# A convolution with residual and group normalization: from one image in four parities on the full PE array to two images in row parity on four array tiles

## The chip, the cores and the metric

The kernel runs on one core of a Trainium2 chip. The metric is device time in microseconds of one execution, lower is better; "span" is the profiled execution from first to last instruction and is some 1.8 us shorter than the time. PE is the matmul engine (its weight loads are counted apart, as PEld), DVE the vector engine, ACT the scalar engine, POOL the general engine, and the DMA queues move data between memory and the core. A record is one instruction in the trace; a call of `nc.tensor.matmul` in FP32 leaves two (192 for 96 calls in the kernel before). A group is the work for one block of rows of an image or a pair, and a group is called warm when PE's granted clock reads 1.00 during it and a record of 396 columns takes 0.333 us. The chain of waits is the work that ended last, followed back from the last instruction.

## The reference

```python
def _gn(v, G=16, eps=1e-5):          # mean and variance over 2 channels x H x W
    g = v.reshape(B_, G, C_ // G, H_, W_)
    return ((g - m) / jnp.sqrt(s + eps)).reshape(v.shape)

# x: (8, 32, 128, 128) f32, weight: (32, 32, 3, 3), bias: (32,)
x = x + conv(_gn(x), weight, bias)   # convolution by FFT of size 256
```

The FFT convolution crops its result at an offset, so that only a corner of about 66 x 66 outputs per image is a real convolution; elsewhere the output is x plus bias. All of x must still be read and written: 16.8 MB each way.

## The kernel before

The host permutes x so that one image fills 128 partitions as 4 parities (row and column odd or even) x 32 channels, 64 x 64 elements each. Four 128x128 matrices per group of 11 rows do the convolution. Statistics of an image are taken 1 to 2 images ahead.

```python
def multiply(img, n):
    ps = ps_conv.tile([P, ROWS, N], F32, ...)              # 11 x 33 = 363 columns
    for k in range(4):
        top, left = n * ROWS + k // 2, k % 2
        nc.tensor.matmul(ps, w_sb[:, k, :], g[:, top : top + ROWS, left : left + N], ...)
    return ps
...
take_stats(1, 0, NSTAT)
aggregate(1)
for img in range(B):
    more, yet_more = img + 1 < B, img + 2 < B
    ps = multiply(img, 0)
    if more:
        group_mean(img + 1)          # small matmul, its operand is ready long since
        deviations(img + 1)
    add(img, 0, ps)
    if yet_more:
        take_stats(img + 2, 0, NSTAT // 2)     # two images ahead
    ps = multiply(img, 1)
    if more:
        group_variance(img + 1)      # second small matmul
        normalize(img + 1)
        store(img + 1, N, H)
    add(img, 1, ps)
    if yet_more:
        take_stats(img + 2, NSTAT // 2, NSTAT)
        aggregate(img + 2)
    ps = multiply(img, 2)
    add(img, 2, ps)
    store(img, 0, N)
```

Of the kernel before, what the change touches and what calls it, by code (L numbers as in the profile page):

```python
# [21 lines left out]
F32 = mybir.dt.float32  # L25
AF = mybir.ActivationFunctionType
ALU = mybir.AluOpType

P = 128
EPS = 1e-5  # L30
FFT = 256
STATS = 8


@with_exitstack
def conv_preact_kernel(
    ctx: ExitStack,
    tc: tile.TileContext,
    x: bass.AP,
    weight: bass.AP,  # L40
    bias: bass.AP,
    out: bass.AP,
):
    nc = tc.nc

    B, _, H, W = x.shape
    C = P // 4
    LO = (FFT - 2 * H) // 4 - 1
    N = H - LO
    ROWS = 11  # L50
    NCHUNK = N // ROWS
    NSTAT = H // STATS

    cpool = ctx.enter_context(tc.tile_pool(name="const", bufs=1))
    xpool = ctx.enter_context(tc.tile_pool(name="x", bufs=1))
    spool = ctx.enter_context(tc.tile_pool(name="small", bufs=2))
    ps_conv = ctx.enter_context(tc.tile_pool(name="ps_conv", bufs=6, space=bass.MemoryType.PSUM))
    ps_stat = ctx.enter_context(tc.tile_pool(name="ps_stat", bufs=1, space=bass.MemoryType.PSUM))


    xts = [xpool.tile([P, H, W], F32, name=f"x{img}") for img in range(B)]
    w_sb = cpool.tile([P, 4, P], F32, name="w_sb")
    bias_sb = cpool.tile([P, 1], F32, name="bias_sb")
    for img in range(B):
        parts = 4 if img == 0 else 2
        for k in range(parts):
            rows = slice(k * H // parts, (k + 1) * H // parts)
            nc.sync.dma_start(xts[img][:, rows, :], x[img, :, rows, :])  # L68
        if img == 0:
            nc.sync.dma_start(w_sb, weight)  # L70
            nc.scalar.dma_start(bias_sb, bias)


    pair = cpool.tile([P, P // 2, 2], F32, name="pair")
    nc.gpsimd.memset(pair, 0.125)
    nc.gpsimd.affine_select(  # L76
        out=pair, in_=pair, pattern=[[-2, P // 2], [0, 2]], base=0,
        channel_multiplier=1, compare_op=ALU.is_ge, fill=0.0,
    )
    nc.gpsimd.affine_select(  # L80
        out=pair, in_=pair, pattern=[[2, P // 2], [0, 2]], base=1,
        channel_multiplier=-1, compare_op=ALU.is_ge, fill=0.0,
    )
    pair2 = pair.rearrange("p a b -> p (a b)")
    avg = cpool.tile([P, P], F32, name="avg")
    nc.vector.tensor_add(avg[:, 0 : 2 * C], pair2[:, 0 : 2 * C], pair2[:, 2 * C : 4 * C])  # L86
    nc.vector.tensor_add(avg[:, 2 * C : 3 * C], avg[:, 0:C], avg[:, C : 2 * C])
    for k in (0, 1, 3):
        nc.vector.tensor_copy(avg[:, k * C : (k + 1) * C], avg[:, 2 * C : 3 * C])
    eps = cpool.tile([P, 1], F32, name="eps")  # L90
    nc.vector.memset(eps, EPS * FFT * FFT)

    warm = cpool.tile([P, 1], F32, name="warm")
    nc.scalar.activation(warm, eps, AF.Sqrt)  # L94


    gs = []
    for k in range(2):
        g = cpool.tile([P, N + 1, N + 1], F32, name=f"g{k}")
        nc.gpsimd.memset(g[:, N : N + 1, :], 0.0)  # L100
        nc.gpsimd.memset(g[:, 0:N, N : N + 1], 0.0)
        gs.append(g)

    stats = [cpool.tile([P, NSTAT, 6], F32, name=f"stats{img}") for img in range(B)]
    mvs, ps_ms, ps_vs, means = {}, {}, {}, {}

    def take_stats(img, first, last):
        for s in range(first, last):
            nc.vector.bn_stats(  # L109
                stats[img][:, s, :],  # L110
                xts[img][:, STATS * s : STATS * (s + 1), :].rearrange("p h w -> p (h w)"),
            )

    def aggregate(img):
        mvs[img] = spool.tile([P, 2], F32, tag="mv", bufs=3, name=f"mv{img}")
        nc.vector.bn_aggr(mvs[img], stats[img].rearrange("p n s -> p (n s)"))  # L116

    def group_mean(img):
        ps_ms[img] = ps_stat.tile([P, 1], F32, tag="ps_m", name=f"ps_m{img}")
        nc.tensor.matmul(ps_ms[img], avg, mvs[img][:, 0:1], start=True, stop=True)  # L120

    def deviations(img):

        means[img] = spool.tile([P, 2], F32, tag="mean", name=f"mean{img}")
        nc.vector.tensor_copy(means[img][:, 0:1], ps_ms[img])  # L125
        diff = means[img][:, 1:2]
        nc.vector.tensor_sub(diff, mvs[img][:, 0:1], means[img][:, 0:1])  # L127
        nc.vector.scalar_tensor_tensor(  # L128
            diff, in0=diff, scalar=diff, in1=mvs[img][:, 1:2], op0=ALU.mult, op1=ALU.add
        )  # L130

    def group_variance(img):
        ps_vs[img] = ps_stat.tile([P, 1], F32, tag="ps_v", name=f"ps_v{img}")
        nc.tensor.matmul(ps_vs[img], avg, means[img][:, 1:2], start=True, stop=True)  # L134

    def normalize(img):
        xt, g = xts[img], gs[img % 2]

        std = spool.tile([P, 1], F32, tag="std", name=f"std{img}")
        nc.scalar.activation(std, ps_vs[img], AF.Sqrt, bias=eps, scale=float(FFT * FFT))  # L140
        rstd = spool.tile([P, 2], F32, tag="rstd", name=f"rstd{img}")
        nc.vector.reciprocal(rstd[:, 0:1], std)  # L142
        nc.vector.scalar_tensor_tensor(  # L143
            rstd[:, 1:2], in0=means[img][:, 0:1], scalar=-1.0, in1=rstd[:, 0:1],
            op0=ALU.mult, op1=ALU.mult,
        )
        nc.scalar.activation(  # L147
            g[:, 0:N, 0:N], xt[:, LO:H, LO:W], AF.Identity,
            bias=rstd[:, 1:2], scale=rstd[:, 0:1],
        )  # L150

        low = xt[:, N:H, :].rearrange("p h w -> p (h w)")
        nc.scalar.activation(low, low, AF.Identity, bias=bias_sb)  # L153
        right = xt[:, 0:N, N:W]
        nc.scalar.activation(right, right, AF.Identity, bias=bias_sb)  # L155

    def multiply(img, n):
        g = gs[img % 2]
        ps = ps_conv.tile([P, ROWS, N], F32, tag="ps", name=f"ps{img}_{n}")
        for k in range(4):  # L160
            top, left = n * ROWS + k // 2, k % 2
            nc.tensor.matmul(  # L162
                ps, w_sb[:, k, :], g[:, top : top + ROWS, left : left + N],
                start=(k == 0), stop=(k == 3),
            )
        return ps

    def add(img, n, ps):

        part = xts[img][:, n * ROWS : (n + 1) * ROWS, 0:N]  # L170
        nc.vector.scalar_tensor_tensor(  # L171
            part, in0=ps, scalar=bias_sb, in1=part, op0=ALU.add, op1=ALU.add
        )

    def store(img, first, last):
        nc.sync.dma_start(out[img, :, first:last, :], xts[img][:, first:last, :])

    take_stats(0, 0, NSTAT)
    aggregate(0)
    group_mean(0)  # L180
    deviations(0)
    group_variance(0)
    normalize(0)
    store(0, N, H)
    take_stats(1, 0, NSTAT)
    aggregate(1)
    for img in range(B):
        more, yet_more = img + 1 < B, img + 2 < B
        ps = multiply(img, 0)
        if more:  # L190
            group_mean(img + 1)
            deviations(img + 1)
        add(img, 0, ps)
        if yet_more:
            take_stats(img + 2, 0, NSTAT // 2)
        ps = multiply(img, 1)
        if more:
            group_variance(img + 1)
            normalize(img + 1)
            store(img + 1, N, H)  # L200
        add(img, 1, ps)
        if yet_more:
            take_stats(img + 2, NSTAT // 2, NSTAT)
            aggregate(img + 2)
        ps = multiply(img, 2)
        add(img, 2, ps)
        store(img, 0, N)


# [36 lines left out]
```

## Time and profile before

| | before |
|---|---|
| time, median (range) | 89.98 us (89.44 to 90.11, 3 runs) |
| span of the profiled run | 88.2 us |
| PE busy, DVE busy, ACT busy | 67.2, 60.6, 37.9 us |
| PE's convolution on the chain of waits | from 16.4 to 82.4 us without a break |
| moved by DMA | 33.84 MB, 384 GB/s over the span, some 424 GB/s in the middle |

How to read it: the busy times alone suggest that PE has a quarter of the span to spare. The chain of waits says otherwise: from 16.4 us on the convolution never stops, and what PE does not use lies before and behind it. The lines, and how full the transfers are, are in the prediction.

### The profile page before, as it was taken

To read this page: it belongs to the slowest core of one execution; us is meant where nothing else is said; L and a number is where in the kernel's file an instruction comes from. 1 tells how busy PE (TensorE), PEld (TensorE's weight loads), DVE (VectorE), ACT (ScalarE), POOL (GpSimd) and SP (SyncE) were. 2 spreads that over 40 slices of the span, in tenths; PEclk is the share of its full clock that TensorE was granted. 3 is DMA by queue.
4 is the path that set the end of the run, shared out by engine and by line. 5 is a ranking of instruction groups with operands and counts; after the bars stand their busy time and mean duration, and the time that the engine had idled before them with its cause. 6 is when DMAs were issued, how large, how long until landed. Compare 5 with 4: busy or idle time off the path is not lost.

```text
span 88.2 us, 744 instructions
## 1 busy us (share of the span) xinstructions
PE 67.2 (76%) x224; PEld 41.5 (47%) x224; DVE 60.6 (69%) x142; ACT 37.9 (43%) x34; POOL 2.1 (2%) x11
## 2 busy tenths in 40 slices
PE   0000022599999999999999999999999999999300
PEld 0000022356665665666566556656664666666000
DVE  0308965992999799979979997998899723222200
ACT  4200003970049517922980594189139707910000
POOL 6200000000000000000000000000000000000000
PEclk9999999999999999999999999999999999999997
DMA  1679999999999999999999999999999999799392
GB/s 20 160 283 420 441 416 416 424 416 416 416 424 428 428 420 413 424 416 424 405 415 436 428 422 420 422 439 428 423 427 419 437 431 426 306 401 424 153 391 100
DMA packets 5186, 33.84 MB, mean 384 GB/s; under 512 B 704, under 2 KB 704, under 8 KB 2368
## 3 DMA queue, kind: packets, MB, share of 16 engines
q1 hardware_dynamic: 5040, 33.82, 93.1%
q10 hardware_dynamic: 144, 0.00, 0.1%
q8 instruction: 1, 0.02, 0.1%
q14 instruction: 1, 0.01, 0.0%
HBM read 17.04 MB, written 16.78 MB: 384 GB/s over the span
## 4 chain that ended last, share of the span: by engine, by line
PE 76%; DMA 8%; DVE 7%; ACT 2%; issue 1%; SPq 0%; DVEq 0%
PE ps L162 73%; DMA x<-x_dram 8%; DVE stats L109 4%; PE ps_m L120 2%; PE ps_v L134 2%; ACT g L147 1%; DVE x L171 1%; DVE mv L116 0%; SPq L68 0%; ACT std L140 0%; DVE mean L128 0%; DVE rstd L142 0%; DVE rstd L143 0%; DVE mean L127 0%; DVE mean L125 0%
## 5 line engine op out<-in xcount | busy, mean ns | idle before, releaser
L162 PE MATMUL ps<-g,w_sb 128*128 128x363 f32 x192 | 65.9, 493 | 2.1 <-ACT g L147 2.1
L162 PEld LDWEIGHTS ps<-g,w_sb 128*128 128x128 f32 x192 | 36.1, 197 | 23.5 <-ACT g L147 5.2
L109 DVE BATCH_NORM_STATS2 stats<-x 128x6 f32<-128x512 f32 x64 | 39.5, 679 | 3.4 <-DMA x<-x_dram 3.4
L171 DVE SCALAR_TENSOR_TENSOR x<-ps,bias_sb,x 128x363 f32<-128x363 f32 x24 | 13.8, 576 | 7.0 <-PE ps L162 7.0
L153 ACT ACTIVATE x<-x,bias_sb 128x1984 f32<-128x1984 f32 x8 | 15.6, 1949 | 0.3
L140 ACT ACTIVATE std<-ps_v,eps 128x1 f32<-128x1 f32 x8 | 2.1, 261 | 31.4 <-PE ps_v L134 31.4
L147 ACT ACTIVATE g<-x,rstd 128x1089 f32<-128x1089 f32 x8 | 10.4, 1305 | 5.8 <-DVE rstd L143 4.9
L120 PE MATMUL ps_m<-mv,avg 128*128 128x1 f32 x16 | 2.7, 236 | 12.4 <-DVE mv L116 12.4
L120 PEld LDWEIGHTS ps_m<-mv,avg 128*128 128x128 f32 x16 | 3.4, 222 | 14.4 <-DVE mv L116 12.4
L155 ACT ACTIVATE x<-x,bias_sb 128x1023 f32<-128x1023 f32 x8 | 9.1, 1132 | 0.0
L125 DVE COPY mean<-ps_m 128x1 f32<-128x1 f32 x8 | 1.3, 158 | 5.5 <-PE ps_m L120 5.5
L134 PEld LDWEIGHTS ps_v<-mean,avg 128*128 128x128 f32 x16 | 3.1, 204 | 2.4 <-DVE mean L128 0.8
L116 DVE BATCH_NORM_AGGREGATE mv<-stats 128x2 f32<-128x48 f32 x8 | 3.0, 372 | 0.3
L142 DVE RECIPROCAL rstd<-std 128x1 f32<-128x1 f32 x8 | 1.2, 150 | 2.8 <-ACT std L140 2.8
L134 PE MATMUL ps_v<-mean,avg 128*128 128x1 f32 x16 | 2.5, 227 | 0.7 <-DVE mean L128 0.7
L86 DVE TENSOR_TENSOR avg<-pair 128x64 f32<-128x64 f32 x1 | 0.2, 226 | 2.6 <-POOL pair L80 2.6
L128 DVE SCALAR_TENSOR_TENSOR mean<-mean,mv 128x1 f32<-128x1 f32 x8 | 1.8, 220 | 0.3
L94 ACT ACT_TABLE_LOAD x1 | 1.3, 1283 | 1.2 <-PEq L234 1.2
L127 DVE TENSOR_TENSOR mean<-mv,mean 128x1 f32<-128x1 f32 x8 | 1.3, 159 | 0.3
L143 DVE SCALAR_TENSOR_TENSOR rstd<-mean,rstd 128x1 f32<-128x1 f32 x8 | 1.3, 160 | 0.3
L76 POOL TENSOR_SCALAR_AFFINE_SELECT pair<-pair 128x128 f32<-128x128 f32 x1 | 0.7, 706 | 0.1
L80 POOL TENSOR_SCALAR_AFFINE_SELECT pair<-pair 128x128 f32<-128x128 f32 x1 | 0.7, 706 | 0.1
(11 smaller groups left out, 1.9 us busy)
## 6 DMA issues: line engine op xcount, KB each, us to landing
x<-x_dram SPq DMA_DIRECT2D x14, 1024.0 KB, 19.0
out_dram<-x SPq DMA_DIRECT2D x8, 1056.0 KB, 14.2
out_dram<-x SPq DMA_DIRECT2D x8, 992.0 KB, 15.2
x<-x_dram SPq DMA_DIRECT2D x4, 512.0 KB, 7.3
w_sb<-weight_dram SPq DMA_DIRECT2D x1, 256.0 KB, 8.6
bias_sb<-bias_dram ACTq DMA_DIRECT2D x1, 0.5 KB, 6.0
```

Of the source, the lines that this page charges most:

```text
L94: nc.scalar.activation(warm, eps, AF.Sqrt)
L109: nc.vector.bn_stats(stats[img][:, s, :], xts[img][:, STATS * s : STATS * (s + 1), :].rearrange("p h w -> p (h w)"),)
L116: nc.vector.bn_aggr(mvs[img], stats[img].rearrange("p n s -> p (n s)"))
L120: nc.tensor.matmul(ps_ms[img], avg, mvs[img][:, 0:1], start=True, stop=True)
L128: nc.vector.scalar_tensor_tensor(diff, in0=diff, scalar=diff, in1=mvs[img][:, 1:2], op0=ALU.mult, op1=ALU.add)
L134: nc.tensor.matmul(ps_vs[img], avg, means[img][:, 1:2], start=True, stop=True)
L140: nc.scalar.activation(std, ps_vs[img], AF.Sqrt, bias=eps, scale=float(FFT * FFT))
L147: nc.scalar.activation(g[:, 0:N, 0:N], xt[:, LO:H, LO:W], AF.Identity, bias=rstd[:, 1:2], scale=rstd[:, 0:1],)
L153: nc.scalar.activation(low, low, AF.Identity, bias=bias_sb)
L155: nc.scalar.activation(right, right, AF.Identity, bias=bias_sb)
L162: nc.tensor.matmul(ps, w_sb[:, k, :], g[:, top : top + ROWS, left : left + N], start=(k == 0), stop=(k == 3),)
L171: nc.vector.scalar_tensor_tensor(part, in0=ps, scalar=bias_sb, in1=part, op0=ALU.add, op1=ALU.add)
```

## The change

The intent is to spend less of PE on zeros. With row parity alone, a 3x3 kernel needs six 64x64 matrices, and four 64x64 matrices are to run at a time on quarters of the array: two images (column halves of the array) by two blocks of rows (row halves). One matmul of five columns replaces two small ones, and the bias comes in one transfer with the weights. Work is now by pairs of images.

```diff
-    for k in range(4):
-        top, left = n * ROWS + k // 2, k % 2
-        nc.tensor.matmul(ps, w_sb[:, k, :], g[:, top : top + ROWS, left : left + N], ...)
+    for k in range(2 * K):
+        dr, b = k // K, k % K
+        for i in range(2):               # row half of the array: block of rows
+            for s in range(2):           # column half: image of the pair
+                nc.tensor.matmul(
+                    ps[HP * s : HP * (s + 1), i, 0 : rows * N],          # 396 or 330 columns
+                    w_sb[HP * i : HP * (i + 1), HP * k : HP * (k + 1)],
+                    g[HP * i : HP * (i + 1), s, r + dr : r + dr + rows, K - 1 - b : K - 1 - b + N],
+                    start=(k == 0), stop=(k == 2 * K - 1),
+                )
...
+    for pair in range(NPAIR):
+        last = pair + 1 == NPAIR
+        ps = multiply(pair, 0)
+        if not last:
+            take_stats(pair + 1)         # all 16 of them here
+            rstd = moments(pair + 1)     # with the one small matmul
+            normalize(pair + 1, rstd)
+            add_bias(pair + 1)
+        add(pair, 0, ps)
+        for n in range(1, len(SPLIT)):
+            add(pair, n, multiply(pair, n))
+        store(pair, 0, U)
+        if not last:
+            store(pair + 1, U, H)
...
-            nc.sync.dma_start(w_sb, weight)
-            nc.scalar.dma_start(bias_sb, bias)
+            nc.sync.dma_start(wb_sb, wb)
```

## The prediction

> **What bounds the kernel now.** I read the strip of forty slices first, then the chain of waits, then the groups of instructions, then stretches of the timeline. The strip says which engines have holes:
>
> ```profile
> PE   0000022599999999999999999999999999999300
> DVE  0308965992999799979979997998899723222200
> DMA  1679999999999999999999999999999999799392
> GB/s 20 160 283 420 441 416 416 424 416 416 416 424 428 428 420 413 424 416 424 405 415 436 428 422 420 422 439 428 423 427 419 437 431 426 306 401 424 153 391 100
> ```
>
> Two rows are full at the same time. PE is at nine tenths from slice 8 to slice 36, and the transfers run at some 424 GB/s from slice 3 to slice 33. So two limits lie close together: 33.84 MB at 424 GB/s is 80 us of pure transfer, and with about 4 us lost in the first three slices the transfers alone need some 85 us of a span of 88.2. The chain of waits names the one that ended last:
>
> ```profile
> PE 76%; DMA 8%; DVE 7%; ACT 2%; issue 1%; SPq 0%; DVEq 0%
> ...
> 16.38 5.21 PE ps L162 x8
> ...
> 53.83 2.55 PE ps L162 x8
> ...
> 72.50 9.89 PE ps L162 x32
> ```
>
> It is PE's convolution, without a break from 16.4 to 82.4 us. Each matmul of the program is two records (192 for 96 calls). The last row gives the rate: 9.89/32 = 0.309 us for a record of 363 columns, 0.851 ns per column. The first row, 0.65 us each, is the same work at half that rate. The costs of the other work are in the groups:
>
> ```profile
> L162 PE MATMUL ps<-g,w_sb 128*128 128x363 f32 x192 | 65.9, 493 | 2.1 <-ACT g L147 2.1
> L109 DVE BATCH_NORM_STATS2 stats<-x 128x6 f32<-128x512 f32 x64 | 39.5, 679 | 3.4 <-DMA x<-x_dram 3.4
> L171 DVE SCALAR_TENSOR_TENSOR x<-ps,bias_sb,x 128x363 f32<-128x363 f32 x24 | 13.8, 576 | 7.0 <-PE ps L162 7.0
> L153 ACT ACTIVATE x<-x,bias_sb 128x1984 f32<-128x1984 f32 x8 | 15.6, 1949 | 0.3
> L147 ACT ACTIVATE g<-x,rstd 128x1089 f32<-128x1089 f32 x8 | 10.4, 1305 | 5.8 <-DVE rstd L143 4.9
> ```
>
> The column before the bar's right half is busy time and mean; what follows is idle time. DVE waited only 7.0 us for PE, because the statistics run two images ahead: when PE reaches the small matmul of the next image, its operand is there. That look-ahead is what the change gives up. The first statistics, and the end, in the timeline and in a table of stretches:
>
> ```profile
> 8.10 3.87 DVE L109 BATCH_NORM_STATS2 stats<-x 128x6 f32<-128x512 f32 x6 [0.23 <-DMA x<-x_dram]
> 12.43 0.58 PE L120 MATMUL ps_m<-mv,avg 128*128 128x1 f32 x2 [12.43 <-DVE mv L116]
> ...
> 82.40:88.20 5.80, 0.00 (x0) 0.00 (x0) 0.60 (x1) 0.00 (x0) 0.00 (x0) 0.90 0.46 192
> ```
>
> The second half-megabyte part had landed at 8.1 us; after PE's last matmul, add and last store take 5.8 us.
>
> [...]
>
> **The change part by part.** The layout halves the wasted multiplications: six 64x64 matrices for two row parities, where before four 128x128 matrices served four parities. A pair of images now needs 3 groups of 24 calls, each on a quarter of the array: 396, 396 and 330 columns. Scaled by the 0.851 ns, a record is 0.337 or 0.281 us, and each call is still two records. If quarters shared nothing, a pair would take 48 x (0.337 + 0.337 + 0.281) = 45.8 us, four pairs 183 us. With perfect overlap of four tiles a quarter of this, 11.45 us a pair, 46 us in all, against 66 us of convolution before.
>
> I do not expect four. The calls are issued tile by tile, and both records of a call are for the same tile. [...] That makes an overlap of two: one record time per call, 24 x 0.337 = 8.1 us for a group of 396, 6.7 us for one of 330, 22.9 us a pair, about 92 us in all. This is my main choice.
>
> The second thing is the order. The instruction order of the changed kernel shows on PE: first group of pair p, the small matmul of pair p+1, then the second and third group. On DVE: all 16 statistics of pair p+1, its moments, then the six adds of pair p. So PE's second group waits for 16 statistics, and the next statistics wait for the third group's add. This is a loop of both engines in which neither hides the other.
>
> Start: the first megabyte lands at 8.1 us as before. The 16 statistics take 16 x 0.617 = 9.9 us (39.5/64), about the pace of the transfers, so to 18.0. Moments: aggregate 0.43 (0.37 before for half the elements), scaling 0.2, matmul 0.6, copy 0.2, three squares 0.7, root 0.3, reciprocal and product 0.4: 2.8 us, to 20.8. It saves one matmul round of the old chain and adds two vector steps. Normalization: two ACT pieces of 1188 and 1056 elements, about 1.4 + 1.3 us from the 1.305 for 1089, two on DVE beside them: PE starts at 23.5, where it was 16.4. That is 7 us later, because a pair is twice the data of an image.
>
> The loop: DVE is free at 23.0; statistics, aggregate and scaling end at 33.5. The first group ends at 34.2 (8.1 plus 2.6 at half clock). Small matmul 0.3, second and third group 14.8: 49.3. Two adds of 330 columns: 1.2 us, DVE free at 50.5. Next round: statistics to 61.1, PE having finished its group at 57.4; then 0.3 + 14.8 + 1.2 to 77.4. Third: 88.0, then PE to 103.1. The last pair's 22.9 us follow at once, since normalization (ACT 5.3 us) lies under the two groups: 126.0. Tail: 5.8, plus 0.6 for the second add, plus 1.15 MB more in the last store (2.9 us at 391 GB/s): 135.3. Time over span was 89.98 - 88.2 = 1.8: 137 us. PE's idle stretches of 3.7 us before the small matmul may bring the half clock back, up to 2.6 us each for two rounds: 142 at most. The bias behind the weights removes one transfer of 0.5 KB; worth nothing, since nobody on the chain waits for it.
>
> **The rivals.** First, all four tiles overlap[...]. [...] Then PE's groups are 4.05, 4.05 and 3.4 us, but the loop stays: a round is 10.6 + 0.3 + 7.45 + 1.2 = 19.6 us, DVE is free at 42.6 and 62.2, the last small matmul ends at 73.1, and 7.45 + 11.45 + 9.3 + 1.8 follow: 103 us. With half clock after each idle stretch[...], 108. Second, FP32 tiles do not overlap at all: PE alone needs 183 us, with start and tail about 220. Nothing in this profile excludes it. Third, DVE is the bound with PE free: 23.0 + two rounds of 16.3 (9.9 + 2.8 + 3.6 for adds) to 55.6, the last 12.7 of statistics and moments, ACT 5.3, convolution 11.45, tail and offset 11.1: 96 us. So even the best PE leaves it slower. Fourth, the changed kernel is bound by transfers: the same bytes need some 85 us of span, so 87 us at best. For this speak the full transfer row; against it, the loop, which makes stores late and leaves holes.
>
> **Range and chances.** Overlap of two at one half, of four at a quarter to three tenths, something between at a tenth, none or worse at some 15%. I predict 136 us. The range 103 to 148 takes in two, four and what lies between. A gain over 2% needs under 88.2 us, just above the transfer limit and below the DVE case: 3%. Within 2%: 3%. Slower: 94%.
>
> **What would show it right or wrong.** The timeline of PE: 48 records of a 396 group in 8.1 us (two), 4 us (four) or 16 us (none). DVE's idle time before the adds, for PE, near 14 us a pair instead of 7.0 us in all. PE idle before each small matmul, released by the scaled means. PE's first convolution at 23.5 us. Holes in the transfer row after about 45 us, when the loads are over. If statistics are faster than 0.617 us, or the tiles overlap fully, I am too high; if tiles wait for weight loads, too low.

The sum came to 135.3 us of span, 137 us of time, at most 142 us with the half clock in two rounds, and 136 us was predicted. The overlap of two stands as my estimate without evidence: the kernel before has no 64x64 matmul in its trace, so nothing measured spoke for two, four or none. "Half clock" stands there for the eight records of 0.65 us at 16.38 us, after PE's waits at the start, against 0.309 us later; the granted clock reads 1.00 in that stretch too. The 2.6 us are half of their 5.21 us. That it comes back after idle stretches was an estimate then; the result below shows where it did. In the rival's sum for 108 us these are stretches of some 6.5 us (10.6 less 4.05).

## The result, and the profile after

The changed kernel takes 105.84 us (105.19 to 106.59, 4 runs), against 90.03 us of the kernel before in the same rounds: a ratio of 1.178, interval 1.168 to 1.188. Ratios are the mean time of one kernel's fast runs over that of the other's of the same rounds, so not quite the ratio of the medians. It is slower, as predicted, but by 16 us and not by 46.

The strip of forty slices of the changed kernel (a slice is now 2.6 us):

```profile
PE   0000002299709999920089999500499999995000
DVE  1389996899996242999954229999660332243000
DMA  2999999999999999899999102999600029996792
GB/s 60 421 421 415 475 412 412 462 437 402 412 456 424 424 405 405 328 422 434 430 431 411 59 0 108 431 418 422 250 0 0 0 94 384 414 451 285 323 431 108
```

PE and DVE now have holes, and the holes alternate: where PE is at 0, DVE is at 9, and DVE falls to 6 and less while PE does its second and third groups (slices 12 to 15, for one). The row of transfers has two stretches near zero, slices 22 to 24 and 29 to 32, when the loads are over (the last lands at 46.1 us) and stores wait for results. Nothing is full any more; the kernel lost to waits what it saved in work.

The chain of waits, its engine shares, and one round of it (start, duration, what):

```profile
DVE 46%; PE 40%; DMA 5%; issue 1%; DVEq 0%; ACT 0%
...
41.78 9.51 DVE stats L121 x16
...
51.31 0.60 DVE mv L129
...
52.22 0.59 PE ps_m L132 x2
52.81 9.50 PE ps L186 x96
...
62.33 1.03 DVE x L202 x2
63.36 9.51 DVE stats L121 x16
```

This is the loop of both engines that the prediction describes: sixteen statistics, aggregate (0.60), small matmul, second and third group (96 records in 9.50 us), two adds, and the next statistics. A round is 63.36 - 41.78 = 21.6 us for a pair; two images before took 16.0 us (2 x 8.0, from the starts of successive images in the chain before). The groups of instructions say who waited:

```profile
L186 PE MATMUL ps<-g,wb_sb 64*64 64x396 f32 (+1 forms) x576 | 54.6, 534 | 3.2 <-ACT g L166 3.2
L202 DVE SCALAR_TENSOR_TENSOR x<-ps,wb_sb,x 128x396 f32<-128x396 f32 (+1 forms) x24 | 13.4, 602 | 23.9 <-PE ps L186 23.9
L132 PE MATMUL ps_m<-mv,avg 128*128 128x5 f32 x8 | 2.2, 340 | 34.8 <-DVE mv L130 34.8
```

The last numbers of each row are idle time and its cause. DVE waited 23.9 us for PE before the adds (7.0 before), and PE waited 34.8 us for the scaled means before the small matmul (12.4 before, all of it at the start). 16.3 of the 34.8 are the start; the other three waits are 3.2, 7.6 and 7.6 us. With each of the three the granted clock fell to 0.50: from 32.7 to 36.2, 49.8 to 56.6 and 70.3 to 77.1 us, where PE works again from 31.07, 52.22 and 73.80 us. The first group is slow too, 7.71 us for 48 records, but there the clock reads 1.00, as at the start of the kernel before.

Now the step that I got wrong. Stretches of 1.33 us, that is four times the 0.333 us that a record of 396 columns takes here, in a warm 396 group of the changed kernel. A group is called warm when PE's granted clock reads 1.00 during it and a record of 396 columns takes 0.333 us. A line gives the length, the busy time of PE, of its weight loads and of DVE, the granted clock, the share of the DMA engines and GB/s. The counts in brackets are instructions that touch the stretch, and the second count is that of weight loads, one for each record:

```profile
83.06:84.39 1.33, 1.33 (x20) 0.57 (x16) 1.03 (x2) 1.00 0.04 12
84.39:85.72 1.33, 1.33 (x20) 0.57 (x16) 0.00 (x0) 1.00 0.50 209
```

Sixteen weight loads in four record times (1.33 us): four records per record time, an overlap of four, where the prediction said two. The interval between the adds of two warm 396 groups gives the same:

```profile
87.30 1.17 DVE L202 SCALAR_TENSOR_TENSOR x<-ps,wb_sb,x 128x396 f32<-128x396 f32 x2 [2.96 <-PE ps L186]
91.29 1.17 DVE L202 SCALAR_TENSOR_TENSOR x<-ps,wb_sb,x 128x396 f32<-128x396 f32 x2 [2.82 <-PE ps L186]
```

These are 91.29 - 87.30 = 3.99 us for 48 records, against 48 x 0.333 = 16.0 us without overlap.

### The profile page after: what moved, and what is told of

Read it like the earlier page. It is cut to its first block, busy times and chain, and to the rows that moved or that the text cites. A ratio compares the mean times of both kernels' runs of the same rounds, so it can differ in the third digit from the quotient of the medians.

```text
span 103.5 us, 1428 instructions
## 1 busy us (share of the span) xinstructions
PE 56.6 (55%) x584; PEld 25.2 (24%) x584; DVE 62.4 (60%) x132; ACT 43.0 (42%) x28; POOL 6.4 (6%) x11
## 4 chain that ended last, share of the span: by engine, by line
DVE 46%; PE 40%; DMA 5%; issue 1%; DVEq 0%; ACT 0%
PE ps L186 38%; DVE stats L121 37%; DMA x<-x_dram 5%; DVE x L202 3%; DVE mv L129 2%; PE ps_m L132 2%; DVE g L162 2%; DVE mv L130 1%; DVE m L137 1%; DVEq L265 0%; ACT std L143 0%; DVE m L134 0%; DVE rstd L145 0%; DVE rstd L146 0%; DVEq L162 0%
## 5 line engine op out<-in xcount | busy, mean ns | idle before, releaser
L186 PE MATMUL ps<-g,wb_sb 64*64 64x396 f32 (+1 forms) x576 | 54.6, 534 | 3.2 <-ACT g L166 3.2
L186 PEld LDWEIGHTS ps<-g,wb_sb 64*64 64x64 f32 x576 | 23.4, 149 | 31.9 <-issue 21.5
L202 DVE SCALAR_TENSOR_TENSOR x<-ps,wb_sb,x 128x396 f32<-128x396 f32 (+1 forms) x24 | 13.4, 602 | 23.9 <-PE ps L186 23.9
L132 PE MATMUL ps_m<-mv,avg 128*128 128x5 f32 x8 | 2.2, 340 | 34.8 <-DVE mv L130 34.8
L166 ACT ACTIVATE g<-x,rstd 64x1188 f32<-64x1188 f32 (+1 forms) x14 | 18.5, 1323 | 2.1 <-DVE rstd L146 1.9
L174 ACT ACTIVATE x<-x,wb_sb 128x3840 f32<-128x3840 f32 x4 | 14.0, 3497 | 0.1
L176 ACT ACTIVATE x<-x,wb_sb 128x2108 f32<-128x2108 f32 x4 | 8.2, 2041 | 0.0
L97 POOL MEMSET g<- 128x2448 f32 x2 | 4.2, 2132 | 0.0
L137 DVE SCALAR_TENSOR_TENSOR m<-m 128x1 f32<-128x1 f32 x12 | 2.6, 219 | 0.4
L129 DVE BATCH_NORM_AGGREGATE mv<-stats 128x2 f32<-128x96 f32 x4 | 2.4, 589 | 0.1
## 6 DMA issues: line engine op xcount, KB each, us to landing
wb_sb<-wb_dram SPq DMA_DIRECT2D x1, 192.5 KB, 10.6
```

The source lines that it names most:

```text
L97: nc.gpsimd.memset(g, 0.0)
L129: nc.vector.bn_aggr(mv[:, 0:2], stats[pair].rearrange("p n s -> p (n s)"))
L132: nc.tensor.matmul(ps_m, avg, mv, start=True, stop=True)
L137: nc.vector.scalar_tensor_tensor(m[:, 1:2], in0=m[:, k : k + 1], scalar=m[:, k : k + 1], in1=m[:, 1:2], op0=ALU.mult, op1=ALU.add,)
L166: nc.scalar.activation(to, of, AF.Identity, bias=rstd[src, 1:2], scale=rstd[src, 0:1])
L174: nc.scalar.activation(low, low, AF.Identity, bias=bias_sb)
```

## The experiments

Fourteen kernels ran. On one core "slow" is said of a run over 1.5% above the fastest of its kernel, and kernels whose PE idles much varied more here (125.93 to 132.29 us in one of them, 100.11 to 100.43 us in the one with PE kept busy). Where their stretches of half clock fall may differ from run to run; with one trace for each kernel this is not shown. Where too few fast runs are left, no ratio is given. The kernel before took 89.39 to 89.79 us (medians) in the rounds of these experiments.

### Which order of the calls lets array tiles overlap?

**Tile by tile.** All six matrices of one tile, then the next tile.

```diff
-        for k in range(2 * K):
-            dr, b = k // K, k % K
-            for i in range(2):
-                for s in range(2):
+        for i in range(2):
+            for s in range(2):
+                for k in range(2 * K):
+                    dr, b = k // K, k % K
```

> The 24 calls of a group in the order tile by tile (all six matrices of one array tile, then the next tile) instead of matrix by matrix. Which calls stand next to each other is all that changes. Theory A, [...]the look-ahead is long enough to hide any order: a warm 396 group stays near 4.0 us and the time near 106 us. Theory B,[...] no overlap within a tile, a 396 group near 16 us and the time near 200 us. Theory C, [...]only within a limited look-ahead: in between, a 396 group of 6 to 12 us, and the time 120 to 170 us. I expect C.

178.23 us, ratio 1.98; the profiled run fell in the slow state (201 us), so its counts are used only in a stretch where PE's clock was granted in full:

```profile
112.23:113.57 1.34, 1.34 (x7) 0.65 (x7) 0.32 (x1) 1.00 0.43 182
113.57:114.90 1.33, 1.33 (x8) 0.59 (x5) 0.00 (x0) 1.00 1.01 419
```

Five to seven weight loads instead of sixteen, so an overlap of about 1.5. The gaps between the starts of successive records of that group, in us, one line for one tile's turn of twelve records (read from the trace's single records):

```
0.33 0.33 0.33 0.33 0.33   0.01 0.33   0.06 0.27   0.06 0.28   0.06
0.33 0.33 0.33 0.33 0.33   0.01 0.33   0.06 0.28   0.06 0.28   0.06
```

Eight record times per tile instead of twelve: four times two records start nearly together. I read those as the last four records of one tile beside the first four of the next; the trace does not name a record's tile. By this reading a new tile got its turn when the tile before had four records left. The run shows neither a group without overlap (16 us) nor a look-ahead that hides any order (4.0 us). Theory C holds in kind (a warm 396 group took 181.62 - 170.75 = 10.87 us between its adds); its 120 to 170 us were missed, partly because PE ran at half clock for long stretches (records 0.66 us apart instead of 0.33). In this slow run no long idle stretch stood before two of them: by the trace's single records the clock fell at 86.9 and at 124.4 us, not 2.5 us after PE had stopped for only 0.42 us, and stayed at half for 10 and 31 us while PE worked on (in the chain 98 records from 85.29 us took 26.21 us, and 238 from 123.38 us took 67.11 us). Why is not shown.

**Two tiles, then the other two.** `for i` outside, then `for k`, then `for s`.

> The 24 calls of a group with the two row halves one after the other: all six matrices of the first 64 rows, alternating between its two column tiles, then the same for the other 64 rows. Two tiles stand next to each other in the order, never four. Theory: the overlap is what a near neighbour in the order allows, so it is two here; a warm 396 group takes 8 us, and the rest of my prediction's loop can be judged: with an overlap of two it said 137 us, less 3.4 us because PE starts at 20.1 us and not 23.5: 133 to 139 us. Rival: the look-ahead reaches past it and overlaps the row halves too, nearer to 106 us.

131.84 us (125.93 to 132.29; one run of four counts as fast, the profiled one of 125.93). The expected 133 to 139 us were missed by 7 us in the fast run, and a slow run comes within 1 us of them for the wrong reason: a warm group took not 8 but 5.45 us (110.99 - 105.54 between its adds in the trace), an overlap of 2.9, and other groups ran at half clock (weight loads 0.66 us apart instead of 0.33, from 54.8 to 64.1 us, in 144 records without a break), which hid part of the difference. The counts of weight loads alternate:

```profile
104.90:106.23 1.33, 1.33 (x14) 0.56 (x8) 0.69 (x2) 1.00 0.98 419
106.23:107.57 1.34, 1.34 (x16) 0.73 (x16) 0.48 (x1) 1.00 0.93 393
```

Eight, then sixteen: for four record times two tiles run alone, then for four the other two run beside them, and so on. By the same reading the next tiles started when four records were left on each tile before them.

**Blocks of two and of three calls.** This is a test of the count of four.

```diff
-        for k in range(2 * K):
-            for i in range(2):
-                for s in range(2):
+        for k0 in range(0, 2 * K, block):      # block = 2 or 3
+            for i in range(2):
+                for s in range(2):
+                    for k in range(k0, k0 + block):
```

> Each array tile gets two calls (four records) before the next tile's turn; in the changed kernel it gets one call. From the two reordered runs I read that a new tile's first record starts when the tile before has four records left. Theory four: four records per tile can wait, so blocks of four records still overlap by four; a warm 396 group takes 4.0 us and the time is 106 us as in the changed kernel. Theory two calls apart is already too far: a group of 5 us or more, the time 112 us or more.

> The same with blocks of three calls (six records). Theory four: each new tile's block is let in two record times after the one before it, so four blocks of six records take eight record times instead of six; a warm 396 group takes 16 record times of 0.333 us, 5.3 us, a 330 group 4.4 us, and the time is 120 to 130 us as in the run with two tiles. Rival, the look-ahead counts in another way: 4.0 us or over 6 us.

Blocks of two: 108.18 us (106.48 to 108.39), the profiled fast run 106.48, level with the changed kernel. Blocks of three: 125.42 us (123.82 to 126.40). Stretches of four record times in a 396 group, first with blocks of two, then with blocks of three:

```profile
89.93:91.26 1.33, 1.33 (x21) 1.05 (x17) 0.00 (x0) 1.00 1.04 445
```

```profile
105.03:106.36 1.33, 1.33 (x15) 0.84 (x12) 0.00 (x0) 1.00 0.87 370
```

Seventeen (one of them on the edge) against twelve: overlap four and overlap three. The group times, between the adds, are 92.59 - 88.60 = 3.99 us and 109.47 - 103.69 = 5.78 us; 4.0 and 5.3 were predicted. As an estimate of mine from these runs, four records pending per tile, the running one among them, fit all five orders. Counted by hand, with records let in one by one in the order of the calls and at most four on a tile, a group comes out at 12 record times in the changed kernel and with blocks of two, 16 with blocks of three and with two tiles, 32 tile by tile. That is 4.0, 5.3 and 10.7 us by the 0.333 us; measured are 3.99 and 3.99, 5.78 and 5.45, 10.87 us. With three or five pending, blocks of three would by the same count take 8.0 or 4.0 us. The 0.5 us over the 5.3 is not explained, and nothing in a trace shows the records that wait.

### What does the order of PE's work cost?

**All three groups first**, so that the small matmul comes last.

```diff
-        ps = multiply(pair, 0)
+        groups = [multiply(pair, n) for n in range(3)]
         if not last:
             take_stats(pair + 1)
...
-        add(pair, 0, ps)
-        for n in range(1, len(SPLIT)):
-            add(pair, n, multiply(pair, n))
+        for n in range(3):
+            add(pair, n, groups[n])
```

> PE gets all three groups of a pair before the small matmul of the next pair; nothing else moves. Theory loop (the small matmul behind 16 statistics holds back groups two and three, and the adds behind them hold back the next statistics): DVE's wait for PE before the adds falls from 23.9 us to near the 6 us of the last pair, a round falls from 21.4 us to some 16.3 us, and the time falls by about 10 us, to 95 to 97 us. Theory half clock (PE is slow after its idle stretches, order is secondary): at most 6 us less, about 100 us. If tiles or transfers bound it: no change from 106 us.

106.63 us, ratio 1.188: nothing gained. By the expectation the theory of the loop falls here. The waits show what happened (total, times, longest):

```profile
PE ps L186 <- ACT g L166: 16.2, 7, 3.2
...
DVE m L134 <- PE ps_m L132: 14.8, 4, 5.3
DVE x L202 <- PE ps L186: 13.1, 3, 8.1
```

The wait before the adds fell from 23.9 to 13.1 us, all of it now in the last pair. But DVE now waits 14.8 us for the small matmul, which stands behind the third group in PE's order, and PE waits 16.2 us for the normalization behind it. A loop is still there, another one: groups, small matmul, moments, normalization, groups. My theory was right on the loop of the changed kernel and wrong in that breaking it at this place leaves none.

**Small matmul after the second group.** The same edit with `range(2)` ahead of the statistics, and the third group behind the normalization.

> The small matmul of the next pair stands on PE after the second group, neither after the first (changed kernel) nor after the third (the run with all groups first). Statistics are ready 10.5 us after their start, when the second group has just ended. Theory loop: neither engine then waits long for the other; a round falls from 21.4 us to 17 or 18 us and the time to 95 to 98 us. Rival, the half clock after idling is all that is left to gain: still 105 us.

97.24 us, ratio 1.085, all four runs within about 1%. A round is 17.3 us (66.73 - 49.39 between small matmuls). The statistics end some 2 us before the second group does, so neither waits long; the wait of DVE for the small matmul, 14.8 us with all groups first, is

```profile
DVE m L134 <- PE ps_m L132: 6.4, 4, 2.3
```

One matmul's place in the order is worth 8.6 us.

**Look-ahead taken from the kernel before.** All eight statistics of the next image stand behind the first group of this one, and there are none two images ahead:

```diff
-    take_stats(1, 0, NSTAT)
-    aggregate(1)
     for img in range(B):
         ps = multiply(img, 0)
         if more:
+            take_stats(img + 1, 0, NSTAT)
+            aggregate(img + 1)
             group_mean(img + 1)
...
-        if yet_more:
-            take_stats(img + 2, ...)     # both halves
```

> The kernel before with its look-ahead taken away: statistics of the next image stand on DVE after the first group of this image, as in the changed kernel, and the second group waits for them. Theory loop: a round per image grows from 8.0 us to some 11.3 us (5.3 statistics and aggregate, 0.9 small matmul and deviations, two groups of 2.5, one add), 7 rounds, so 110 to 116 us, more with the half clock. Rival, the order is harmless and the 64x64 tiles cost it: 90 us.

122.03 us; the only run that counts as fast took 116.83 us, the profiled one 121.13 (slow, so its length is not compared). Its wait for the small matmul, against one wait of 12.4 us in the kernel before:

```profile
PE ps_m L120 <- DVE mv L116: 32.8, 7, 12.4
```

The array layout is the old one here; the order alone, with the half clock that comes with it, costs the old kernel 27 us in its fast run. The rounds in the trace are 11.3 to 14.3 us (from starts of successive small matmuls): the short ones are as worked out ahead, and in the long ones the second group ran partly at half clock (3.9 to 5.2 us instead of 2.7).

### What does the half clock cost?

**PE kept busy.** Idle matmuls into a spare bank, between first group and small matmul.

```diff
         ps = multiply(pair, 0)
+        keep_busy(pair)     # 4, 10, 10, 0 calls of 128x128 by 396 columns, result unused
```

> Between the first group and the small matmul PE does 4, 10 and 10 idle full-array matmuls of 396 columns into a spare bank, some 2.7, 6.7 and 6.7 us that lie in its wait for the statistics. Theory half clock: groups two and three of the first three pairs take 7.4 us instead of 9.3 to 9.5, and the time falls by 3 x 2 us, to about 100 us. Theory loop: the same 6 us are gained since the groups lie on the loop, but the rounds still hold 10.5 us of statistics plus the groups, 19.3 us each. If the slow stretch after idling is not cured by work, or the work delays the small matmul: 106 us or more.

100.19 us (100.11 to 100.43), ratio 1.121: 5.6 us less, as expected. In the chain the two groups of a round take

```profile
50.96 7.58 PE ps L187 x96
```

instead of 9.50 us, and the mean granted clock of the profiled run is 0.964 instead of 0.889. More work on PE makes the kernel faster here; the loop stays, with a round of 19.45 us (59.59 - 40.14).

### What made the start faster than predicted?

**The bias alone again**, and **small first parts**, in the changed kernel; **large first parts** in the kernel before.

```diff
+            nc.scalar.dma_start(bias_sb, bias)        # first run: bias as its own transfer
-        parts = 2 if pair else 4
+        parts = 2 if pair else 8                      # second run: 4 KB a partition
-        parts = 4 if img == 0 else 2
+        parts = 2                                     # third run: kernel before, 8 KB
```

> The bias comes again as its own transfer of 128 pieces of 4 bytes, from ACT's queue, as in the kernel before; everything else as changed. The first part of x landed at 5.5 us in the changed kernel; I had predicted 8.1 us for its megabyte. Theory bias: the small transfer slowed the first parts, and the first statistics start 1 to 2.5 us later here, time up by as much, 107 to 108 us. Theory packets: it does nothing, first statistics at 5.5 us, 106 us.

> The first pair is loaded in 8 parts (4 KB a partition and part, as in the kernel before) instead of 4 of 8 KB. Theory packets (4 KB pieces move at 130 to 280 GB/s at the start, 8 KB pieces at 418): the transfer rate from 3 to 6 us falls to about 200 GB/s, the fourth statistics ends later than in the changed kernel and the first convolution starts 1 to 2 us later, time 107 to 108 us. Theory bias: the rate stays at 418 GB/s, the first statistics start 1 us earlier with half the data, time 105 to 106 us.

> The kernel before, with its first image loaded in 2 parts of 8 KB a partition instead of 4 of 4 KB; its bias stays alone. Theory packets: the rate is near 400 GB/s from 3 us on, the whole first image lands near 7 to 8 us instead of 10 us, and the first convolution starts 1 to 2 us before 16.4 us; the time falls by 1 to 2 us, if the transfers don't bound it already. Theory bias: rate 130 to 280 GB/s as before, start not before 16.4 us.

The stretch from 4 to 5 us of the kernel before, the changed kernel, and the changed kernel with the bias alone (the last number is GB/s, the one before it the share of the DMA engines):

```profile
4.00:5.00 1.00, 0.00 (x0) 0.00 (x0) 0.00 (x0) 0.00 (x0) 0.00 (x0) 1.00 0.63 148
```

```profile
4.00:5.00 1.00, 0.00 (x0) 0.00 (x0) 0.00 (x0) 0.00 (x0) 1.00 (x1) 1.00 0.99 410
```

```profile
4.00:5.00 1.00, 0.00 (x0) 0.00 (x0) 0.00 (x0) 0.00 (x0) 1.00 (x1) 1.00 0.82 270
```

With the bias alone the first statistics start at 6.51 us instead of 5.51, and the time is 107.31 us; small parts with the bias behind the weights took 105.97 us on the same chip. Small parts start the first statistics earlier, at 4.42 us, but these then wait 1.45 us for data, and the first convolution starts 0.6 us later than in the changed kernel. So the transfer of 128 pieces of 4 bytes costs 1 us of the start, as its expectation said, and the small parts some half microsecond, where each of the two theories hit half. The kernel before with large parts takes 89.05 us, ratio 1.000 (0.991 to 1.009): its convolution ends 1 us earlier, but the expected gain of 1 to 2 us isn't shown. Why its rate from 5 to 6 us is still only 279 GB/s I take to be its bias, which was not tried alone there.

### Is there a version that beats both?

**Second group and busy**: the small matmul after the second group, and four idle matmuls after the third. **Combined**: besides that, the last pair is normalized by ACT and DVE together and its last rows are stored group by group. **All by group**: stores of all pairs in this way.

```diff
+        groups.append(multiply(pair, 2))
+        if not last:
+            keep_busy(pair)                       # 4 calls, into PE's wait for the normalization
...
-                if pair == 0 and s == 1:
+                if pair in (0, NPAIR - 1) and s == 1:
...
             add(pair, n, groups[n])
+            for i in range(2):                    # combined: last pair alone
+                store(pair, PART * i + r, PART * i + r + rows)
```

> Of the combined attempt only two parts: the small matmul after the second group, and the four idle matmuls after the third. It tells apart where the 6.3 us from 97.2 us to the combined 91.0 us came from. Theory clock: nearly all, since the rounds in the run without idle matmuls took 17.4 us against 15.7 us here, and the last pair's convolution 13.9 against 11.5 us: 91.5 to 93 us. Theory tail (the last pair's shared normalization and its stores by group): 94 us or more.

> The attempt to beat both: small matmul after the second group, four idle matmuls after the third to keep the clock up, the last pair normalized by ACT and DVE together, the last pair's rows stored group by group. DVE is then nearly always busy until the last moments at some 66 us; normalization 2.7, convolution 11.4, tail 5 to 6: span 86 to 89, time 88 to 91 us, near the 85 us that the transfers need. If the loop still holds a wait that I don't see: 93 us or more.

> The combined attempt with the stores of all pairs issued group by group, so that transfers begin earlier. Theory transfers: the hole in the transfer row at 67 to 71 us (76 and 125 GB/s) is partly filled and the time falls by 0.5 to 1.5 us, to 89.5 to 90.5 us, level with the kernel before. Rival: smaller pieces cost as much as they gain, 91 us or more.

Second group and busy: 92.54 us, ratio 1.031, in the range of its clock theory: the four idle matmuls are the only difference from 97.24 us. Combined: 90.97 us, ratio 1.017 (1.009 to 1.025). All by group: 89.39 us, against 89.79 us of the kernel before in the same rounds, ratio 0.997 (0.991 to 1.002): level. The transfers of the last:

```profile
DMA  3899999899999999999899999999998799999960
GB/s 52 355 423 423 423 449 464 374 471 419 427 438 389 471 404 427 427 419 367 309 416 396 407 410 449 450 388 396 438 449 344 281 387 455 407 407 376 389 269 13
```

The long holes are gone, and with them the room: 33.84 MB at some 420 GB/s are 80 us, and start and end add the rest. That the transfers set this end for both layouts is argued and not shown; PE's chain is nearly unbroken in both too (here from 20.2 to 81.4 us, idle matmuls included). No version was found that is clearly faster than the kernel before.

In one row, with the array tiles as in the changed kernel throughout: 105.84 us; 97.24 by the place of the small matmul; 92.54 by the idle matmuls; 90.97 by the last pair's normalization and stores; 89.39 by all stores group by group. So a better order, the clock and the last steps are enough to win back the whole 16 us with the tiles as they are. The runs are of different rounds, but the kernel before took 89.58 to 90.03 us in all of them.

## Why the prediction was right or wrong

- **Direction and loop: right.** The change of order was read from the two instruction orders, and the loop is what the chain shows. The round is shorter (21.2 and 21.6 us against 27.5 and 26.9) by the term below. That the order and not the tiles costs the time is shown from three sides: moving one matmul gives 8.6 us back, the old layout without its look-ahead takes 117 us in its fast run, and the same tiles in a better order reach the time of the kernel before.
- **Overlap of two: wrong, and it's the step that failed.** The prediction let one call of 396 columns take one record time, so a group 8.1 us and a pair 22.9 us. Measured are 3.99 us for a warm group and 11.3 us for the last pair (three groups, from the adds at 83.31 to the end of PE at 94.60). The two was an estimate without evidence. By my count from the runs four records per tile fit while other tiles start; a call has two; so in this order nothing waits. Blocks of two calls still overlap by four (3.99 us a group) and blocks of three by three (5.78 us). In my timeline the error is 5 to 6 us in each of two rounds and 17.4 us from the last statistics to the end of PE (48.6 against 31.2 us), nearly all of the 30 us by which I was too high.
- **The rival was right.** Overlap of four with the loop was put at 103 us, and at 108 us with the half clock after each idle stretch; 105.84 us lies between, and keeping PE busy gives 100.19 us. I gave it a quarter to three tenths, and two one half. Both of its sums carry the late start; with DVE free at 20.5 and not 23.0 us they come to some 100.6 and 105.8 us, almost what was measured with and without idle matmuls. What stood against it was only my assumption, without evidence, that a call's second record keeps the next tile waiting.
- **Start: 3.4 us too late.** The convolution starts at 20.1 us, not 23.5. Of this, 2.6 us are the statistics, which end at 15.4 and not 18.0; another 1.3 us come from PE starting after the first of ACT's two pieces and not after both (1.4 us against 2.7), and the moments took 0.4 us longer than the 2.8. I took the landing of the first megabyte at 8.1 us from the kernel before; its slow start (148 GB/s from 4 to 5 us, against 410) belonged to its own transfers. "Worth nothing" for the bias was wrong by 1 us.
- **Half clock: right in kind.** The reserve was 2.6 us each for two rounds, 5.2 us; the measured value is 5.6 us in all, over three waits, so some 1.9 us each. That the sums nearly agree is luck.
- **Transfer holes, waits before the small matmul: right in kind.** The loads end near 45 us as foretold, but the holes begin at 57 us, because stores fill the row until then. DVE's wait before the adds was put at 14 us a pair and is 23.9 us in all, some 5.3 us in each of three rounds and 7.9 in the last pair, by the shorter groups.

## What to carry to other kernels

When work is cut into larger pieces, write down for each engine the order of what it does and follow one round: a small matmul behind a long chain on another engine makes both stand, and its place in the order alone was worth 8.6 us here. Before counting on an overlap of array tiles, or ruling it out, look at how many records in a row go to one tile (two or four, 3.99 us a group here; six, 5.78 us; twelve, 10.87 us). And where the transfers need 85 of 88 us (an estimate from 33.84 MB at 424 GB/s and 4 us lost at the start), a change of the arithmetic can lose much and win little.
